# A conditional ternary feed-forward kernel: x and the result kept block by block in HBM, one row per partition

## The chip, the cores and the metric

The kernel runs on one core of one Trainium2 chip. The core has five engines with a queue each: TensorE (PE, with its weight loads shown as PEld), VectorE (DVE), ScalarE (ACT), GpSimd (POOL) and SyncE (SP). Sixteen DMA engines move data between HBM, the memory outside the core, and SBUF, the memory of 128 partitions inside it; PSUM holds the sums of matmuls. The metric is the device time of one execution in microseconds (us), the median over several runs. Arranging the inputs and the result on the host isn't part of it.

## The reference

x has 128 samples of 64 channels and 512 tokens in float32, 16.8 MB. Each sample picks one 64 x 64 matrix from a table of 200, and then all go through a feed-forward layer with ternary weights; the result is quantized with one scale over the whole tensor and added to x.

```python
w = weights[conditions]                          # (128, 64, 64)
z = einsum('bct,bcd->bdt', x, w)                 # per sample
W1q, W2q = ternarize(W1), ternarize(W2)          # alpha * sign(W) where |W| > 0.05 max|W|
h = gelu(einsum('bsd,hd->bsh', z, W1q) + b1)     # 512 -> 2048
y = einsum('bsd,hd->bsh', h, W2q) + b2           # 2048 -> 512
scale = max(abs(y)) / 7 + 1e-8                   # one number for all of y
q = clip(round(y / scale), -7, 7) * scale
return x + q
```

Since the scale needs the largest element of all of y, no part of the result can be written before the last block's y is known.

## The kernel before, in words

Two samples fill the 128 partitions (2 x 64 channels): a pair. Four pairs make a block, so there are 16 blocks of 1 MB of x, 8 KB per partition. A tile of x in SBUF is 128 partitions x 4 pairs x 512 tokens, and half a block is two pairs.

The kernel has three stages. At the start, SP loads both weight matrices (8 KB rows per partition, `nat1`, `nat2`) with block 0 of x between them; thresholds and ternary weights are made, while POOL gathers the conditional matrices row by row (`fetch`) and lays them into a block-diagonal `diag` (`place`). In the middle, block after block, PE mixes each pair of the next block with `diag` and runs the two layers over 16 hidden chunks; blocks 2 to 12 use a scheme with seven products in place of eight (`seven`). The y of blocks 0 to 14 stays in SBUF (`ys`), that of block 15 in PSUM. At the end, the scale is found, and for each half of each block ACT rounds y to int8, DVE multiplies by the scale and adds x, in place, and POOL issues the store.

x is therefore read twice: once for the layers and once for the final addition. The functions that load it all issue on SP:

- `load_x` (line 104): a whole block into a tile of the pool `big`, as two loads of half a block each.
- `half_x` (line 112) and `split_x` (line 118): half a block into a tile of the pool `half`.
- `quarter_x` (line 743): one pair, for blocks 2 to 13, into one of two slots of `x_quarters`.
- `lend` (line 819): one pair of blocks 3 and 4, for the final addition, into the room of a weight tile that is no longer read.

For the final addition, blocks 0 to 2 are loaded during the last block's layers, 3 and 4 by `lend`, 5 and 6 by `load_x`, 7 to 9 by `split_x`, and 10 to 15 by `load_x` inside the final loop. The order of issue on every engine is the order of the program (`InOrder`, line 55, is the line that all records carry). What decides when one of these loads starts is the tile it is given: SP waits there until the earlier user of the room has finished, be it DVE, PE or the store of a y. The names x_blk and out_blk (lines 98 and 99) are views of x and of the result in which one partition's row of a block is four pieces of 2 KB that lie 256 KB apart.

Of the kernel before, what the change touches and what calls it, by code (L numbers as in the profile page):

```python
# [40 lines left out]
P = 128  # L41
# [17 lines left out]
def tile_cond_ternary_ffn(  # L59
# [12 lines left out]
    pe, act, dve, pool, sp = (  # L72
        InOrder(tc, e) for e in (nc.tensor, nc.scalar, nc.vector, nc.gpsimd, nc.sync)
    )
    B, C, T = x.shape
    S, _, D = weights.shape
    NT = T // P
    NH = W1.shape[1]
    assert 2 * C == P and 2 * D == P and C == D and W1.shape == (P, NH, NT, P)
    PAIRS = 4  # L80
    BLK = PAIRS * P
    NB = B // (2 * PAIRS)
    NG = 4
    GH = NH // NG
    WCH = GH * T
# [9 lines left out]
    ps_h = ctx.enter_context(tc.tile_pool(name="ps_h", bufs=2, space=PSUM))  # L95
    ps_y = ctx.enter_context(tc.tile_pool(name="ps_y", bufs=1, space=PSUM))

    x_blk = x.rearrange("(n j p) c t -> n (p c) j t", j=PAIRS, p=2)
    out_blk = out.rearrange("(n j p) c t -> n (p c) j t", j=PAIRS, p=2)

    def pair_of_pairs(h):
        return slice(h * PAIRS // 2, (h + 1) * PAIRS // 2)

    def load_x(n):

        xt = big.tile([P, PAIRS, T], F32, tag="big", name=f"xt_{n}")
        for h in range(2):
            js = pair_of_pairs(h)
            sp.dma_start(out=xt[:, js, :], in_=x_blk[n][:, js, :])
        return [xt[:, pair_of_pairs(h), :] for h in range(2)]  # L110

    def half_x(n, h):

        xt = half.tile([P, PAIRS // 2, T], F32, tag="half", name=f"xt_{n}_{h}")
        sp.dma_start(out=xt, in_=x_blk[n][:, pair_of_pairs(h), :])
        return xt

    def split_x(n):

        return [half_x(n, h) for h in range(2)]  # L120
# [14 lines left out]
    for g in range(NG):  # L135
        w = big.tile([P, GH, T], F32, tag="big", name=f"nat1_{g}")
        for ks in PIECES[g]:
            sp.dma_start(out=w[:, ks, :], in_=W1f[:, g * GH :, :][:, ks, :])
        nat1.append(w)
    x_next = load_x(0)  # L140
    b1t = const.tile([P, NH], F32)
    sp.dma_start(out=b1t, in_=b1)
    for g in range(NG):
# [57 lines left out]
    def parts(n):  # L201
        return [big.tile([P, NT, BLK], F32R, tag="big", name=f"x{k}_{n}") for k in range(2)]
# [54 lines left out]
    def flat(w):  # L257
        return w.rearrange("p a b -> p (a b)")
# [115 lines left out]

    ymax = const.tile([P, NB + 1, PAIRS], F32)
    alpha = {}
# [12 lines left out]
    def widen2(n, hc):  # L389
        if n == 0 and hc < NH - LAG:  # L390
            w = w2f[hc % 4]
        elif n == NB - 1 and hc == NH - 1:

# [241 lines left out]

    w1t = big.tile([P, NH, T], F8, tag="big", name="w1t")
    x_next = load_x(1)

    def kept(t, g, tiles):
# [3 lines left out]
    for hc in range(NH - LAG):  # L643
# [21 lines left out]
        if hc in (5, 7, 9, 11):  # L665
            j = (hc - 5) // 2
# [3 lines left out]
    x_next, two_next, fetched = [], [], []  # L670
# [10 lines left out]
    extra = {}  # L681
# [29 lines left out]
    def parts7(n):  # L711

        return (
            big.tile([P, 2, NT, HALF], F32R, tag="big", name=f"xb_{n}"),
            [big.tile([P, 4, 2, HALF], F32R, tag="big", name=f"xt{k}_{n}") for k in range(2)],
            half.tile([P, 2, 2, HALF], F32R, tag="half", name=f"xl_{n}"),
        )
# [24 lines left out]

    def quarter_x(n, j):

        sp.dma_start(out=extra["x"][:, j % 2, :], in_=x_blk[n][:, j, :])

    def product(out, w, b, first):
        for c in range(2):
# [65 lines left out]

    steps = [(n, hc) for n in range(NB) for hc in range(NH)]
    again = []
    dying = [flat(t).bitcast(F32).rearrange("p (j t) -> p j t", j=PAIRS) for t in (w1t, w2t)]

    def lend(t, n, hc):

        if n == NB - 1 and hc % (NH // PAIRS) == NH // PAIRS - 1:
            j = hc // (NH // PAIRS)
            sp.dma_start(out=dying[t][:, j, :], in_=x_blk[3 + t][:, j, :])

    def eight(s):

        n, hc = steps[s]
        if s + 1 < len(steps):
            ahead = steps[s + 1]
            if ahead[0] not in SEVEN:  # L830
                widen1(*ahead)
                lend(0, *ahead)
            else:
                for g in (2, 3, 0):
                    widen7(0, g)
        widen2(*steps[s + 1 - LAG])
        lend(1, *steps[s + 1 - LAG])
        if n + 1 < NB:
            if hc == 0:
                if n + 1 == SEVEN[0]:  # L840
                    extra["x"] = half.tile([P, 2, T], F32, tag="half", name="x_quarters")
                    for j in range(2):
                        quarter_x(n + 1, j)
                else:
                    x_next.append(load_x(n + 1) if n + 1 < NB - 1 else split_x(n + 1))
                two_next.append(parts7(n + 1) if n + 1 in SEVEN else parts(n + 1))
            if 2 <= hc < 2 + PAIRS:
                fetched.append(fetch(n + 1, hc - 2))
            if 7 <= hc < 7 + PAIRS:
                place(hc - 7, fetched[hc - 7 - PAIRS])  # L850
# [10 lines left out]
        if n + 1 < NB and 8 <= hc < 8 + PAIRS:  # L861
            j = hc - 8
            if n + 1 in SEVEN:
                condition7(n + 1, j, extra["x"][:, j % 2, :], two_next[-1])()
                if j + 2 < PAIRS:
                    quarter_x(n + 1, j + 2)
            else:
                condition(n + 1, j, pair_of(x_next[-1], j), two_next[-1])
            cond[n + 1] = two_next[-1]
# [17 lines left out]
    def pair(n, k, finish):  # L887
# [14 lines left out]
        def behind(i):  # L902
# [16 lines left out]
            if i == 2:  # L919
                if parting:  # L920
                    parting.pop()()
                if k == 1:
                    quarter_x(n + 1, 0)
                    quarter_x(n + 1, 1)
                if k in (4, 5):
                    quarter_x(n + 1, k - 2)
                widen2(*steps[s])
                if not leaves:
                    widen7(ahead, 2)
# [23 lines left out]
    while s < len(steps):  # L953
        n, hc = steps[s]
# [14 lines left out]
    n = NB - 1  # L969
    widen2(n, NH - 1)  # L970
    lend(1, n, NH - 1)
    again += [[t[:, pair_of_pairs(h), :] for h in range(2)] for t in dying]
    for _ in range(2):
# [30 lines left out]
    for n in range(NB):  # L1004

        while len(xs) < min(AHEAD + 3 * n // 2, NB):
            xs.append(load_x(len(xs)))
        for h in range(2):


            q = quant[:, h * PAIRS // 2 : (h + 1) * PAIRS // 2, :]
            if n < NB - 1:
                y = res = ys[n][:, pair_of_pairs(h), :]
                act.activation(flat(q), flat(y), AF.Identity, scale=inverse)
                dve.scalar_tensor_tensor(
                    flat(y), flat(q), scale, flat(xs[n][h]), ALU.mult, ALU.add
                )
            else:
                res = xs[n][h]
                for k in range(PAIRS // 2):  # L1020
                    y = ypsum[n][h * PAIRS // 2 + k]
                    act.activation(q[:, k, :], y, AF.Identity, scale=inverse)
                    dve.scalar_tensor_tensor(
                        res[:, k, :], q[:, k, :], scale, res[:, k, :], ALU.mult, ALU.add
                    )
            pool.dma_start(out=out_blk[n][:, pair_of_pairs(h), :], in_=res)


_INS = [
# [9 lines left out]

LAID_OUT = {
    "itok_B_1_198": lambda a: a.reshape(-1, 2).T.repeat(P // 2, axis=0),
    "L0_ffn_W1": lambda a: a.reshape(-1, P, a.shape[1] // P, P).transpose(3, 0, 2, 1),
    "L0_ffn_b1": lambda a: a.reshape(-1, P).T,
# [25 lines left out]
```

## Time and profile before

| What | Value |
|---|---|
| Median of 3 runs | 1064.39 us (1062.46 to 1064.63) |
| The profiled execution, time | 1062.89 us |
| The profiled execution, span from first to last instruction | 1061.0 us |
| PE busy | 986.1 us, 93% |
| DVE, ACT, POOL busy | 58%, 58%, 59% |
| DMA, load queue (q1): packets, MB, share of 16 engines | 19872, 42.25, 12.0% |
| DMA, queue of POOL (q0): packets, MB, share of 16 engines | 6656, 18.88, 4.6% |
| Half-block loads of x (36), from issue to landing | 7.2 us, median |
| Stores of y (30), from issue to landing | 12.9 us, median |
| Quarter loads of x (48), from issue to landing | 2.6 us, median |

A row of the profile names the engine, the operation, what it writes and what it reads, with tile numbers left out. Times in a timeline or a chain are us from the span's start, and the number after it is the length in us. In the lines of 40 slices each digit is the busy share of a slice in tenths. The queue q1 carries what SP issues, q0 what POOL issues: gathers, and at the end the stores. A packet is what a DMA engine takes from a queue at a time. The landing of a DMA is when its semaphore has its full count.

### The profile page before, as it was taken

Reading aid. Unit: us, or ns where it says so; the run is one execution under the profiler, and the core shown is the slowest. Engines: PE = TensorE matmul, PEld = TensorE weight load, DVE = VectorE, ACT = ScalarE, POOL = GpSimd, SP = SyncE. Lnnn points to the kernel's source line nnn. Section 1 sums busy time; section 2 is a strip of 40 time slices with the busy share of each in tenths; the row PEclk is TensorE's granted clock in tenths of the full one; section 3 lists DMA queues with packets and bytes.
Section 4 is the critical chain, followed back from the end, with each engine's and each line's share of the span. In section 5 each row is a group of like instructions: output and inputs, shape, how many; then the busy total and the mean of one; then the engine's idle time right before and its main releaser. Section 6 shows DMA issues by size and latency. Waiting matters only on the chain.

```text
span 1061.0 us, 16715 instructions
## 1 busy us (share of the span) xinstructions
PE 986.1 (93%) x5760; PEld 864.0 (81%) x5761; DVE 610.9 (58%) x1078; ACT 611.4 (58%) x1040; POOL 628.2 (59%) x1016
## 2 busy tenths in 40 slices
PE   8999999999999999999999999999999999999400
PEld 5887889999999999999999999999998888888300
DVE  7896645666656565666656565666645224232682
ACT  7974445666666565656666565656655433343481
POOL 6855656676766667676766767676664435333242
PEclk9999999999999999999999999999999999999755
DMA  9100000101000010101000010100001010041899
GB/s 361 57 20 3 23 22 12 34 6 31 15 22 23 14 32 7 39 6 32 15 22 23 14 32 5 40 6 30 16 22 43 3 40 6 1 149 33 301 413 372
DMA packets 26611, 62.20 MB, mean 59 GB/s; under 512 B 3488, under 2 KB 3488, under 8 KB 25760
## 3 DMA queue, kind: packets, MB, share of 16 engines
q1 hardware_dynamic: 19872, 42.25, 12.0%
q0 software_dynamic: 6656, 18.88, 4.6%
q8 instruction: 47, 0.77, 0.3%
q14 instruction: 36, 0.29, 0.1%
HBM read 44.34 MB, written 16.78 MB: 58 GB/s over the span
## 4 chain that ended last, share of the span: by engine, by line
PE 87%; DVE 4%; DMA 3%; ACT 2%; issue 1%; POOL 1%; SPq 1%; POOLq 0%; DVEq 0%; ACTq 0%
PE py L55 42%; PE xy L55 16%; PE ph L55 13%; PE z L55 12%; PE pc L55 5%; DMA xt<-in_x 3%; DVE h L55 1%; DVE y L55 1%; ACT diag L55 1%; DVE terns L55 1%; POOL wg L55 1%; ACT junk L55 1%; SPq L55 1%; DVE junk L55 1%; DMA wg<-in_L_cond_weights,rows 1%
## 5 line engine op out<-in xcount | busy, mean ns | idle before, releaser
L55 PE MATMUL py<-wf,h 128*128 128x512 f32 x2048 | 531.2, 395 | 0.9 <-ACT h L55 0.7
L55 PEld LDWEIGHTS py<-wf,h 128*128 128x128 f32 x2048 | 365.4, 189 | 65.1 <-DVE y L55 2.0
L55 DVE TENSOR_TENSOR h<-ring,h 128x512 fp32r<-128x512 f32 x252 | 194.7, 775 | 182.1 <-ACT h L55 182.1
L55 POOL CAST wf<-w2t 128x512 fp32r<-128x512 fp8e4 x242 | 173.7, 718 | 154.4 <-PE py L55 142.4
L55 ACT ACTIVATE ring<-ring,b1t,alpha_w 128x512 f32<-128x512 f32 x176 | 144.3, 820 | 97.7 <-DVE ring L55 97.7
L55 POOL CAST wf<-w1s 128x256 fp32r<-128x256 fp8e4 (+1 forms) x264 | 134.4, 514 | 108.9 <-PE xy L55 80.5
L55 POOL CAST wf<-w1t 128x256 fp32r<-128x256 fp8e4 (+1 forms) x240 | 156.7, 658 | 56.7 <-PE ph L55 45.2
L55 ACT CAST h<-ring 128x512 fp32r<-128x512 f32 x256 | 158.9, 621 | 8.3
L55 PE MATMUL ph<-x,wf 128*128 128x512 f32 (+1 forms) x648 | 157.6, 388 | 2.8 <-ACT x L55 2.1
L55 PEld LDWEIGHTS ph<-x,wf 128*128 128x128 f32 x648 | 119.8, 188 | 28.8 <-issue 2.5
L55 ACT ACTIVATE ring<-ph,b1t,alpha_w 128x512 f32<-128x512 f32 x80 | 62.3, 779 | 139.6 <-PE ph L55 139.5
L55 DVE TENSOR_TENSOR ring<-xy,ring 128x256 f32<-128x256 f32 (+1 forms) x176 | 97.3, 553 | 64.2 <-PE xy L55 64.2
L55 PEld LDWEIGHTS xy<-xt,wf 128*128 128x128 f32 x704 | 107.6, 189 | 14.1
L55 PE MATMUL xy<-xb,wf 128*128 128x256 f32 x704 | 112.4, 281 | 0.0
L55 PE MATMUL xy<-xt,wf 128*128 128x256 f32 x704 | 111.8, 282 | 0.0
L55 PEld LDWEIGHTS xy<-xb,wf 128*128 128x128 f32 x704 | 102.2, 190 | 7.9
L55 ACT COPY ring<-xy 128x256 f32<-128x256 f32 x176 | 65.1, 370 | 67.7 <-PE xy L55 67.7
L55 PE MATMUL z<-xt,wf 128*128 128x256 f32 x704 | 98.3, 282 | 0.0
L55 ACT COPY ring<-z 128x512 f32<-128x512 f32 x88 | 51.7, 588 | 73.9 <-DVE h L55 72.5
L55 PEld LDWEIGHTS z<-xt,wf 128*128 128x128 f32 x704 | 90.2, 190 | 0.0
L55 DVE TENSOR_TENSOR xt<-x_quarters,xt 128x512 fp32r<-128x512 f32 x44 | 33.8, 768 | 91.1 <-ACT xt L55 91.1
L55 POOL DMA_INDIRECT wg<-in_L_cond_weights,rows x64 | 73.5, 1148 | 11.7 <-issue 4.4
(103 smaller groups left out, 851.4 us busy)
## 6 DMA issues: line engine op xcount, KB each, us to landing
xt<-in_x SPq DMA_DIRECT2D x36, 512.0 KB, 7.2
out<-y POOLq DMA_DIRECT2D x30, 512.0 KB, 12.9
x_quarters<-in_x SPq DMA_DIRECT2D x48, 256.0 KB, 2.6
nat<-in_L_ffn_W SPq DMA_DIRECT2D x6, 1024.0 KB, 10.2
nat<-in_L_ffn_W SPq DMA_DIRECT2D x3, 512.0 KB, 9.0
wg<-in_L_cond_weights,rows POOLq DMA_INDIRECT x64, 2.7
w1t<-in_x SPq DMA_DIRECT2D x4, 256.0 KB, 2.6
w2t<-in_x SPq DMA_DIRECT2D x4, 256.0 KB, 2.6
```

The lines of the kernel that those rows point to most:

```text
L55: return lambda *args, **kw: self._tc.keep_in_program_order(make(*args, **kw))
```

## The change

In HBM, x and the result become arrays of 16 blocks x 128 partitions x 4 pairs x 512 tokens, so that a partition's row of a block is 8 KB in one piece, and that of half a block 4 KB. The host puts x in this order and the result back. In the kernel, `load_x` issues one load of 1 MB in place of two of 512 KB, except for block 0 at the start, where it keeps two (`halves`). The other loads and the stores stay as they are in number and size, with the views replaced by plain indexing. A pair's load now takes 2 KB out of every 8 KB.

```diff
-    B, C, T = x.shape
-    S, _, D = weights.shape
+    S, C, D = weights.shape
+    T = x.shape[-1]
...
-    NB = B // (2 * PAIRS)
+    NB = x.shape[0]
+    B = NB * PAIRS * 2
...
-    x_blk = x.rearrange("(n j p) c t -> n (p c) j t", j=PAIRS, p=2)
-    out_blk = out.rearrange("(n j p) c t -> n (p c) j t", j=PAIRS, p=2)
...
-    def load_x(n):
+    def load_x(n, halves=False):
 
         xt = big.tile([P, PAIRS, T], F32, tag="big", name=f"xt_{n}")
-        for h in range(2):
-            js = pair_of_pairs(h)
-            sp.dma_start(out=xt[:, js, :], in_=x_blk[n][:, js, :])
+        if halves:
+            for h in range(2):
+                js = pair_of_pairs(h)
+                sp.dma_start(out=xt[:, js, :], in_=x[n][:, js, :])
+        else:
+            sp.dma_start(out=xt, in_=x[n])
         return [xt[:, pair_of_pairs(h), :] for h in range(2)]
...
-        sp.dma_start(out=xt, in_=x_blk[n][:, pair_of_pairs(h), :])
+        sp.dma_start(out=xt, in_=x[n][:, pair_of_pairs(h), :])
...
-    x_next = load_x(0)
+    x_next = load_x(0, True)
...
-        sp.dma_start(out=extra["x"][:, j % 2, :], in_=x_blk[n][:, j, :])
+        sp.dma_start(out=extra["x"][:, j % 2, :], in_=x[n][:, j, :])
...
-            sp.dma_start(out=dying[t][:, j, :], in_=x_blk[3 + t][:, j, :])
+            sp.dma_start(out=dying[t][:, j, :], in_=x[3 + t][:, j, :])
...
-            pool.dma_start(out=out_blk[n][:, pair_of_pairs(h), :], in_=res)
+            pool.dma_start(out=out[n][:, pair_of_pairs(h), :], in_=res)
...
+    "x": lambda a: a.reshape(-1, 4, P, a.shape[2]).transpose(0, 2, 1, 3),
...
-    shape = inputs["x"].shape
+    shape = arrays["in_x"].shape
...
-    return r.results[0]["out_0"]
+    return r.results[0]["out_0"].transpose(0, 2, 1, 3).reshape(inputs["x"].shape)
```

## The prediction

> **What bounds the kernel now.** I read the forty slices first, then the chain that ended last, then the stretches of the tail with their DMA traffic by queue.
>
> ```profile
> PE   8999999999999999999999999999999999999400
> DMA  9100000101000010101000010100001010041899
> GB/s 361 57 20 3 23 22 12 34 6 31 15 22 23 14 32 7 39 6 32 15 22 23 14 32 5 40 6 30 16 22 43 3 40 6 1 149 33 301 413 372
> ```
>
> A slice is 26.5 us. TensorE sets the pace in 36 of them while the DMA engines idle; only the first slice and the last three are different. In the last three the DMA engines are the busy ones. The chain shows the change of hands near 988 us, and how it ends:
>
> ```profile
> 987.39 0.63 ACT h L55
> ...
> 1018.95 3.54 SPq L55
> ...
> 1022.60 1.33 SPq L55
> 1023.93 0.04 issue
> 1023.98 27.00 DMA xt<-in_x
> ```
>
> The last load of x takes 27.00 us from its issue to its landing, although 512 KB move in 1.3 us at 400 GB/s: it stands in a queue. SP itself spends 3.54 us and 1.33 us on single issues here (elsewhere 0.33 to 0.46)[...]. So the tail is bounded by bytes over the DMA rate, not by any one transfer. The whole tail (985 to 1062 us), by queue, and then three pure stretches and the mixed one (packets, MB, rate; and per queue the share of the 16 engines):
>
> ```profile
> DMA packets 10738, 28.60 MB, mean 371 GB/s; under 512 B 880, under 2 KB 880, under 8 KB 10736
> q0 software_dynamic: 4608, 16.78, 53.6%
> q1 hardware_dynamic: 6128, 11.80, 41.6%
> ```
>
> Start, 4 to 8 us, weights in 8 KB rows, loads only:
>
> ```profile
> DMA packets 228, 1.66 MB, mean 416 GB/s; under 512 B 22, under 2 KB 22, under 8 KB 28
> ```
>
> 994 to 999.5 us, x in 2 KB rows, loads only; 1020 to 1030 us, loads and stores; 1050 to 1054 us, stores only:
>
> ```profile
> DMA packets 1130, 2.19 MB, mean 397 GB/s; under 512 B 70, under 2 KB 70, under 8 KB 1129
> ...
> DMA packets 1488, 4.15 MB, mean 415 GB/s; under 512 B 123, under 2 KB 123, under 8 KB 1488
> q0 software_dynamic: 743, 2.70, 66.0%
> q1 hardware_dynamic: 745, 1.45, 37.3%
> ...
> DMA packets 462, 1.67 MB, mean 418 GB/s; under 512 B 53, under 2 KB 53, under 8 KB 462
> ```
>
> What to see: 2 KB packets alone run at 397 GB/s, 8 KB packets at 416, stores at 418 (their queue already joins two 2 KB pieces into one 4 KB packet: 32 stores of 0.524 MB in 4,096 packets, the rest of the 4,608 being 32 x 16 completions), and the mixture at 415. In the mixture the two queues take equal numbers of packets, 743 and 745, so bytes go 2.70 to 1.45.
>
> [...] the trace has 416 over 397, 4.8%. [...] the best stretches here stay at 416 to 420.[...] a 256 KB load of x lands in 2.6 us in the trace of before, so the joined loads save no queue time worth counting when transfers overlap.
>
> **The change, part by part.** Every TensorE, DVE, ScalarE and GpSimd instruction stays, in its order. On SP, 11 pairs of 512 KB loads become single 1 MB loads (block 1, block 14, and in the tail blocks 0, 5, 6 and 10 to 15); the other loads stay separate. Rows are 8 KB for these, 4 KB for half-block loads and stores, 2 KB for the quarter loads, now 8 KB apart.
>
> Fit of a packet, from the two load-only rates, per engine (rate/16): 2,048 B in 82.5 ns at 397, 8,192 B in 315.1 ns at 416. Slope 232.6 ns/6,144 B = 37.9 ps/B, overhead 5.0 ns. So 4 KB would run at 409 GB/s, and no packet overhead at all at 422.
>
> (1) Start. Block 0 of x (1 MB, behind 4 MB of weights, 12.9 to 15.5 us) moves at 409 in place of about 380 to 397: up to 0.15 us sooner. The chain there runs through the last gather (landed 13.91 us) and POOL's copies into diag, not through x: 0. If the 4 KB packets delay that gather instead, by two packets at 80 ns, +0.2 us; its bytes mostly passed before block 0's did. I take 0.
>
> (2) Middle. Block 1 is loaded at 42.0 us, lands at about 46.8 and is first read at 64.9; the joined load lands no later than its second half did. The 48 quarter loads land in 2.6 us and no engine but SP waits for one. PE's 18 us of other work is the cover, so the cost is 0; with the cover gone PE would wait the 4.8 us of the landing. What their new 8 KB spacing does to their speed the trace doesn't show as such; weights, in 8 KB rows spaced 32 KB, ran at 416. Even double time (5.2 us) fits in the two steps of 3.6 us between issue and use.
>
> (3) Tail, first loads. Blocks 5, 6 and the first half of 7 (2.62 MB, 0.12 of it moved by 988) are queued by 988.8 us; the next load is issued only at 992.50 us, when PE frees its buffer. Before: 2.19 MB from 988 to 994, mean 365 (the slices fall to 188 GB/s around 991), the last 0.31 MB at 397, so done at 994.8. After: 2.50/0.416 = 6.0 us, at 994.0. Saved 0.8 us if the hollow at 991 goes, 0.3 if it comes again. The load issued at 992.50 moves from about 993.3, so DMA isn't left idle.
>
> (4) The next five half loads (2.62 MB, 4 KB rows): 6.6 us at 397, 6.4 at 409. Saved 0.2.
>
> (5) All the rest, 28.60 - 0.12 - 2.50 - 2.62 = 23.36 MB, from 1001.4 us to the end of movement at about 1058.6, 57.2 us, mean 408. The steady rate is 415.5 and cannot pass 422 by the fit: between 0 and 57.2 x (1 - 415.5/422) = 0.9 us. I take 0.9, as both sides have fewer pieces: loads a quarter, stores half. Two hollows (336 GB/s from 1003 to 1005, 348 from 1012.5 to 1013.5) cost 0.4 and 0.15 us; between 0 and 0.55 is saved. I take 0.55, because the overfull load queue, the likeliest cause, has a quarter of the packets after.
>
> (6) The end. A joined load frees DVE only when both halves are in. Now DVE takes the last half at 1051.07 and the last store is issued at 1052.78; its data still stand behind others until about 1058. Joined alone would put the last store one DVE piece (1.41 us) later, 1054.2, and still ahead of that backlog: cost 0. But the round by packets now gives loads 8 KB against 4 KB, so two thirds of the rate (277 GB/s). Block 10 lands at about 1006; 11 to 15 wait for freed buffers (stores of blocks 0 to 2) and DVE, are queued by about 1017, and land by about 1028 in place of 1051. Late instead are the stores, which fill the queue to the end. POOL waits for its eighth-last store, DVE doesn't wait for POOL. No engine idles the DMA: 0, and if DMA were left idle, up to 1.4 + 0.7 us.
>
> Sum: 0.8 + 0.2 + 0.9 + 0.55 = 2.45 us off the profiled 1062.89 us (span 1061.0 and 1.89 around it). The median, 1064.39, lies 1.5 above that execution; I take the same 2.45 from it: 1061.9 us.
>
> **Rivals.** *Capped mixture:* the two queues already hide each other's packet overhead (415 against 397 alone), so (5) gains only 415 to 418, 0.4 us, and the hollows return: 0.3 + 0.2 + 0.4 = 0.9, 1063.5 us. For it: the mixture stands within 0.7% of stores alone. Against: hollows fall where load packets crowd.
>
> *Slow stores:* a store now writes 4 KB of every 8 KB of the result, where it wrote solid 256 KB runs. 16.78 MB at 418 take 40.1 us. The gain is eaten when stores run at 16.78/42.6 = 394; below 375 the kernel is more than 0.2% slower. At 370, 45.4 us: +5.3 - 2.45 = +2.8, 1067.2 us. For it: nothing in the trace writes so. Against: 8 KB rows read from 32 KB apart ran at 416.
>
> *More gain:* all traffic at 422 moves 28.60 MB in 67.8 us in place of 70.5 (988 to 1058.5), and the ragged end (1057 to 1059.5) sharpens by 1: -3.7, 1060.7 us.
>
> *No effect,* were 8 KB rows cut to 2 KB anyway: excluded, 200 of the packets from 4 to 8 us are of 8 KB.
>
> **How the numbers follow.** Forecast 0.58 (of which 0.05 fall short of the bound), capped mixture 0.21, slow stores 0.14 (0.13 slower, the rest same), more gain 0.07. A measurement of this kernel tells about 0.2%, 2.1 us, from no change. Faster 0.60, same 0.27, slower 0.13. The range leaves out most of the slow stores and the far end of the gain: 1060.3 to 1065.2; the forecast's own is 1060.9 to 1062.6.
>
> **What would show it.** Right: load-only stretches after 988 at 409 to 416 with packets of 8 KB; loads near two thirds of the bytes while both run; block 15 landed by about 1030; no SP issue over 1 us; DVE through by about 1040 and the last 25 us stores alone near 420. Wrong: stores alone below 400, DMA share below 0.9 anywhere from 988 to 1056, PE starting its first ph later than 20.63 us, or a PE wait on x_quarters.

## The result and the profile after

The changed kernel takes 1068.23 us (median of 7 runs, 1066.53 to 1069.81) against 1064.43 us before: a ratio of 1.0038, interval 1.0029 to 1.0048. It is slower by 3.8 us, where 2.5 us less were forecast, and outside the range.

The profiled execution of the changed kernel takes 1068.34 us, span 1066.5. Its forty slices, 26.7 us each:

```profile
PE   8999999999999999999999999999999999999200
DMA  9100000100000000000000000000001010131997
GB/s 363 54 20 3 23 22 8 38 6 30 15 22 23 14 32 14 31 6 31 14 22 23 20 26 14 32 5 30 16 22 44 2 41 5 34 115 40 341 421 311
```

PE still sets the pace in the same 36 slices, and the DMA engines are the busy ones in the first and the last three. The traffic of the tail (985 to 1068 us) has as many bytes in fewer packets: the load queue has 2,160 in place of 6,128. Below stand the whole tail and then, in order, loads alone (994 to 999.5 us), loads and stores (1020 to 1030), stores alone (1050 to 1054):

```profile
DMA packets 6771, 28.61 MB, mean 345 GB/s; under 512 B 752, under 2 KB 752, under 8 KB 5744
q0 software_dynamic: 4608, 16.78, 49.9%
q1 hardware_dynamic: 2160, 11.80, 36.4%
...
DMA packets 549, 2.27 MB, mean 412 GB/s; under 512 B 63, under 2 KB 63, under 8 KB 482
...
DMA packets 768, 4.25 MB, mean 425 GB/s; under 512 B 80, under 2 KB 80, under 8 KB 418
q1 hardware_dynamic: 384, 2.87, 67.8%
q0 software_dynamic: 384, 1.38, 33.8%
...
DMA packets 464, 1.67 MB, mean 418 GB/s; under 512 B 56, under 2 KB 56, under 8 KB 464
```

These rates are as forecast or better: 412 GB/s where the kernel before had 397, 425 where it had 415, 418 where it had 418. The two queues still take equal numbers of packets, 384 each, so loads have two thirds of the bytes. The chain that ended last (start, length, what) has other links, though. It no longer ends in a load of x but in stores waiting for stores:

```profile
1024.48 2.49 DVE y L55 x2
1026.98 0.05 issue
1027.03 14.74 DMA out<-y
...
1042.32 9.44 DMA out<-y
...
1052.28 0.55 POOLq L1071
```

The view's chain stops there, at 1052.83 us, while the DMA engines are still at work.

The last packet of the last store ends at 1061.39 us, and yet the span goes on to 1066.5. What stands there is in the instructions of the program's last line: SP waits for the last landings (EVENT_SEMAPHORE), GpSimd's queue (POOLq) has an instruction that the profile calls DRAIN, then all engines meet. First of the kernel before, then of the changed one (count, shortest/median/longest in ns, first and last start in us):

```profile
L1067 SPq EVENT_SEMAPHORE  x11: 17/28/28, 1059.6 to 1061.0; - x11
L1067 POOLq DRAIN  x3: 40/102/7461, 1052.8 to 1060.8; - x3
```

```profile
L1071 SPq EVENT_SEMAPHORE  x11: 17/28/28, 1061.7 to 1066.4; - x11
L1071 POOLq DRAIN  x3: 40/102/13426, 1052.3 to 1066.2; - x3
```

SP's first wait ends with the last landing, at 1059.6 and 1061.7 us. The long DRAIN begins with the issue of the last store; it took 7.461 us before, to 1060.22, 0.6 us after the landing, and 13.426 us after, to 1065.71, 4.0 us after it.

So the 5.45 us between the two spans part in three:

| Stretch | Before | After | Difference, us |
|---|---|---|---|
| Start to the scale known (start of DVE's reciprocal) | 996.59 | 998.02 | 1.43 |
| From there to the end of the last packet | 62.63 | 63.37 | 0.74 |
| From there to the end of the span | 1.82 | 5.10 | 3.28 |

The first isn't the change's. Between 70 and 110 us the granted TensorE clock was 1.00 in the one profile and 0.96 in the other (half speed for 3.4 us at 86 us). In the 18 profiles of this document the scale is known at 996.4 to 997.1 us in the five without such a dip and at 997.7 to 998.7 us in the 13 with it, in both orders of x. The other two rows make 4.0 us, near the 3.8 of the medians. Of these the 3.28 us behind the last packet are the greater part; the 0.74 us come from one profile each, and the kernel before with one small instruction more (`e8_before_wait` below) has 63.20 us in that row, so the 0.74 is not clear of the spread.

### The profile page after: what moved, and what is told of

Its sections match the earlier page's. It is cut to its first block, busy times and chain, and to the rows that moved or that the text cites. A ratio compares the mean times of both kernels' runs of the same rounds, so it can differ in the third digit from the quotient of the medians.

```text
span 1066.5 us, 16692 instructions
## 1 busy us (share of the span) xinstructions
PE 988.2 (93%) x5760; PEld 865.2 (81%) x5761; DVE 608.9 (57%) x1078; ACT 611.3 (57%) x1040; POOL 620.3 (58%) x1016
## 4 chain that ended last, share of the span: by engine, by line
PE 87%; DVE 5%; DMA 3%; ACT 2%; POOL 1%; issue 1%; POOLq 0%; ACTq 0%; DVEq 0%
PE py L55 41%; PE xy L55 16%; PE ph L55 13%; PE z L55 12%; PE pc L55 5%; DMA out<-y 2%; DVE y L55 2%; ACT diag L55 1%; DVE h L55 1%; DVE terns L55 1%; POOL wg L55 1%; ACT junk L55 1%; DVE junk L55 1%; DMA wg<-in_L_cond_weights,rows 1%; ACT w2t L55 1%
## 5 line engine op out<-in xcount | busy, mean ns | idle before, releaser
L55 PEld LDWEIGHTS py<-wf,h 128*128 128x128 f32 x2048 | 365.5, 189 | 65.2 <-DVE y L55 2.0
```

What stands on the lines that cost most here:

```text
L55: return lambda *args, **kw: self._tc.keep_in_program_order(make(*args, **kw))
```

## The experiments

Theory A blamed the order of loads and stores for the long DRAIN, theory B the 4 KB pieces of a store, theory C the movement of the data itself. A piece is a run of bytes of one partition that lies in one stretch in HBM. "The scale" stands for the moment at which it is known, as in the table.

**Each half of the change alone.** `e1_x_only`:

```diff
-            pool.dma_start(out=out[n][:, pair_of_pairs(h), :], in_=res)
+            pool.dma_start(out=out_blk[n][:, pair_of_pairs(h), :], in_=res)
```

> Only x is kept block by block; the result keeps its old order, so a store is 2 KB pieces again. Theory A (the loss is POOL's last DRAIN, and it is long because the loads come first and a longer queue of stores stands behind the last store's issue): the loads still come first, so the DRAIN stays at 12 us or more, ends over 3 us after the last data packet, and the kernel is 0.3% slower than before, 1067.5 us or more. Theory B (the DRAIN is long because a store is made of 4 KB pieces): DRAIN ends about 1 us after the last packet as before, and the time is 1063 to 1065 us. Theory C (the loss is in the movement of the data, slow stores at an 8 KB pitch): stores alone at 419 GB/s or more, last packet earlier than in the changed kernel by 1 us, and the time within 1 us of before.

`e2_result_only` is the kernel before with only this line (and the result's shape on the host) the other way round.

> Only the result is kept block by block; x keeps its old order and its loads of half a block in 2 KB pieces. Theory A: loads share the rate as before, the queue of stores at the end is as before, the DRAIN ends about 1 us after the last packet, time 1063 to 1065 us. Theory B: the DRAIN ends over 3 us after the last packet, time 1067 us or more. Theory C: last packet later than before by 1 us, time 1065 to 1068 us.

Measured: x alone 1067.01 us, ratio 1.0035 (1.0022 to 1.0047); the result alone 1067.34 us, 1.0028 (1.0018 to 1.0037). Each half loses nearly as much as both, for different reasons. With x alone the DRAIN ends 0.6 us after the last landing, but the last packet comes 65.2 us after the scale, 2.5 later than before: the loads are done early (landed by 1037.2 us), the stores run alone for 26 us, and with 2 KB pieces their rate falls from 413 GB/s (1040 to 1045 us) to 398, 355 and 381 in the next three stretches of 5 us. The changed kernel's 4 KB pieces ran at 416 to 419 from 1040 to 1055 us. The pieces alone don't explain it, since the kernel before ran the same 2 KB pieces alone at 416 to 420 from 1050 to 1056 us; why they turn slow after some 10 us alone stays open. With the result alone the last packet comes at 63.0 and the DRAIN ends 3.98 us after the landing. A fell; of C a part is true for x alone; B seemed to stand (1067.34 us, where it said 1067 or more).

**Stores taken from GpSimd.** The same line with `(sp if n >= 12 else pool)` and later `(sp if n >= 8 else pool)`:

> The changed kernel with the stores of blocks 12 to 15 (the last 8 of 32) issued by SP in place of POOL. Theories A and B: POOL's DRAIN ends before the last data, so the end comes about 1 us after the last packet; 3 to 3.5 us faster than the changed kernel, 1064.5 to 1065.5 us. Theory C: as slow as the changed kernel, 1067.5 to 1069 us.

> The changed kernel with the stores of blocks 8 to 15 (the last 16 of 32) issued by SP, so that POOL's own stores have landed some 10 us before the end. Theory D (POOL's last DRAIN ends a few us after the last landing of POOL's own stores when these are of 4 KB pieces): the DRAIN ends before the last data, the span ends under 2 us after the last packet, and the kernel is 2.5 to 3.5 us faster than the changed one, 1064.5 to 1065.5 us. Theory E (the DRAIN waits for something that comes after all data of the core, whoever issued them): 4 to 5 us after the last packet again, 1067.5 us or more.

With 8 of 32 stores on SP nothing is gained: 1068.04 us, 1.0040 (1.0026 to 1.0054). All three theories had a forecast for this, but the last of GpSimd's stores landed at 1061.20 us, later still than SP's (1057.65), and the DRAIN ended 3.65 us after that. So GpSimd wasn't done early, and the run was no test of A and B. With 16 on SP GpSimd's last store lands at 1047.44 and its DRAIN, begun at 1025.4 and 25.320 us long, is over at 1050.76, 3.32 us after that landing:

```profile
L1071 SPq EVENT_SEMAPHORE  x11: 17/28/28, 1050.5 to 1060.9; - x11
L1071 POOLq DRAIN  x3: 40/102/25320, 1025.4 to 1060.7; - x3
```

The span ends 1.3 us after the last packet, and the time is 1064.31 us, 1.0003 (0.9994 to 1.0012) of before. The data aren't faster for it: 63.3 us from the scale. So it is the end of the DRAIN that costs the 3 to 4 us. That the move to SP brings nothing of its own is checked below with the kernel before.

**A wait ahead of the DRAIN.** Behind the last store, in the changed kernel and in the one before, GpSimd writes one column into the tile that this store reads, so that it has to wait for the store's landing first:

```diff
+    pool.memset(res[:, 0, :1], 0.0)
```

> The changed kernel with one small memset on POOL behind the last store, into the tile that this store reads, so that POOL waits for the store's landing before its DRAIN. If the DRAIN is long because it starts with stores under way and looks for their end only now and then: it is now under 0.5 us, the end is about 1 us after the landing, 1064.5 to 1065.5 us. If the DRAIN is work that POOL still has to do (theory B's kind, in the order of its queue): the memset or the DRAIN ends as late as before, about 4 us after the last packet, 1067.5 to 1069 us.

> The kernel before with the same small memset on POOL behind the last store as in the run that waited before the DRAIN. If a DRAIN behind stores of 2 KB pieces has nothing to wait for: under 0.5 us, and the time is that of before plus 0 to 0.5 us. If a DRAIN begun after the landing takes about 8 us whatever the pieces: 8 us again, 1071 us or more, and the long DRAIN would be the memset's doing or a matter of when it starts, not of the pieces.

The changed kernel with the wait, then the kernel before with it:

```profile
L1072 POOLq DRAIN  x3: 40/102/8055, 1062.3 to 1070.9; - x3
```

```profile
L1068 POOLq DRAIN  x3: 40/102/1277, 1061.7 to 1063.5; - x3
```

Times 1073.24 us, 1.0084 (1.0066 to 1.0101), and 1065.68 us in one run. The memset itself ran in 0.1 us at the landing, and still 8.055 us of DRAIN followed. So the DRAIN isn't idle waiting: here it took 8.055 us with every store landed, and 3.98 us of it were left after the landing in the changed kernel, where it starts early. With the old stores it takes a sixth, 1.277 us.

**Pieces and counts.** Stores cut into quarters of a block (`out[n][:, h * PAIRS // 2 + j, :]`), the last 8 in the old order (this kernel leaves part of the result's rows in another order than it should), those of blocks 0 to 14 joined to a whole block (`out=out[n], in_=ys[n]`), and the kernel before with 16 stores on SP:

> The changed kernel with each store cut into two, one per pair: 64 stores of 256 KB, one piece of 2 KB per partition, 8 KB apart. If the size of a piece (4 KB) makes the DRAIN long: it ends within 0.6 us of the last landing, span end under 2 us after the last packet. If one piece per partition, as against two, makes it long: 4 us after the landing again.

> The changed kernel with the last 8 stores (blocks 12 to 15) in the old order of the result, so of 2 KB pieces, two per partition; these blocks' rows of the result stand in another order than the rest. If the form of the last stores decides the DRAIN: it ends within 0.6 us of the last landing. If what POOL issued before counts too (24 stores of 4 KB pieces): 2 to 4 us after it.

> The changed kernel with the two stores of each of blocks 0 to 14 joined into one of 1 MB, 8 KB pieces; 17 stores in place of 32. If the DRAIN grows with the size of a piece: it ends 6 to 8 us after the last landing. If it grows with the number of stores of pieces of 4 KB or more: 3.3 us or less, as with 16 such stores. The data end about 1 us later than in the changed kernel, since a store starts only when both halves of a block are done.

> The kernel before with the stores of blocks 8 to 15 issued by SP, nothing else changed. With 2 KB pieces POOL's DRAIN was over within 0.6 us of the last landing, so there is nothing to save there: within 1 us of before, 1063.3 to 1065 us. If moving the stores to SP brings something of its own (a better sharing of the DMA engines), it shows here as more than 1 us.

Times: 1069.42, 1069.54 and 1068.58 us in one run each, and 1064.81 us, 1.0003 (0.9995 to 1.0012). From the scale to the last packet they took 66.9, 64.0, 63.7 and 64.1 us; the quarter stores lose their time there and not in the DRAIN. The last of the four also shows that stores on SP bring the kernel before nothing, and it brought theory B down: its stores have 2 KB pieces, and the DRAIN ended 3.32 us after GpSimd's last landing, exactly as with 16 stores of 4 KB pieces (landing at 1036.07 us, DRAIN over at 1039.39):

```profile
L1067 POOLq DRAIN  x3: 40/102/18192, 1021.2 to 1063.7; - x3
```

Sorted by number of DMAs the durations fall on a line. The pieces per engine in the table are an estimate of mine, from the shapes in the kernel and the packets of GpSimd's queue in the traces before and after. Each of the 64 gathers, 128 rows of 256 B, made 16 packets of 2 KB, so eight rows in one, and each of the 32 stores made 128 packets of 4 KB; every one of the 96 DMAs also made 16 packets of 4 B, counted as completions. Shared evenly over 16 engines that makes 8 pieces and a completion, 9, for a gather or a store of one piece per partition, and 17 for a store of two, where a joined packet is counted by its pieces. That joined pieces count singly is assumed; the packets don't show it.

| Run | DMAs of GpSimd | Pieces per engine, completions counted | DRAIN's end after GpSimd's last landing, us | per DMA, ns |
|---|---|---|---|---|
| 16 stores on SP (changed; before) | 80; 80 | 720; 848 | 3.32; 3.32 | 41.5 |
| whole-block stores | 81 | 729 | 3.36 | 41.5 |
| 8 stores on SP | 88 | 792 | 3.65 | 41.5 |
| changed; result only; last 8 old | 96 | 864; 864; 928 | 3.98; 3.98; 3.97 | 41.4 |
| before; x only | 96 | 1,120 | 0.59; 0.59 | - |
| quarter stores | 128 | 1,152 | 0.95 | - |

Theory H is my conjecture from these counts. Call a DMA of GpSimd retired when GpSimd has no more to do for it. H supposes that the DRAIN goes through every DMA that has not been retired, the 64 gathers of the middle too, so that the measured 41.5 ns for each are left after the last landing; and that DMAs are retired earlier only when their pieces fill a room of some 1,020 per engine. By the estimate the kernel before gets there at its 27th store (1,018 pieces before it, 1,035 with it), and its trace has a stall at this store. The timeline of GpSimd in the kernel before (in brackets the idle time ahead):

```profile
1038.94 0.73 POOL L55 DMA_DIRECT2D out<-y  x1 [1.23 <-DMA out<-y]
1042.89 1.46 POOL L55 DMA_DIRECT2D out<-y  x2 [3.22 <-DMA out<-y]
```

The 27th, at 1042.89, goes out 2.60 us after the landing that it waits for (that of the eighth store before it, at 1040.29); others follow theirs by 0.5. With x alone it is the 27th again, by 2.60, and with quarter stores the 50th (1,017 pieces before it, 1,026 with it), by 3.01. The number of DMAs doesn't decide: the stall is at the 91st of GpSimd's DMAs in the first two and at the 114th with quarter stores, while the changed kernel has 96 and no stall. In the kernel before the DMA engines moved 412 to 418 GB/s from 1040 to 1046 us, across the stall, so it cost no movement.

Two more figures of these traces fit. The stores that hadn't landed when the stall began are 13 before and with x alone, 22 with quarter stores; at 41.5 ns each that makes an estimate of 0.54 and 0.91 us for the last column, where 0.59 and 0.95 were measured. And the stall grows with the DMAs that had landed by then: 83 of them and 2.05 us beyond the usual 0.55, 106 of them and 2.46 us, some 24 ns each.

**The count crossed by gathers.** Only the lines below distinguish the two kernels from the changed one, and only the limit, 16 or 20, from each other (not shown: the rest of the gather's arguments and the line that makes the spare tile):

```diff
+    def spare_fetch():
+        if len(spares) < 16:
+            spares.append(1)
+            pool.indirect_dma_start(out=spare[:, :], ...)
...
+                elif k in (6, 7):
+                    spare_fetch()
```

> The changed kernel with 16 more gathers on POOL in the middle (into a spare tile that nothing reads), so 112 DMAs of POOL in place of 96. Theory H (the last DRAIN goes through every DMA of POOL that hasn't been retired, 41.5 ns each after the last landing; they are retired earlier only when their pieces fill a fixed room, between 1,018 and 1,026 pieces per DMA engine by the runs so far): 64 x 9 + 16 x 9 + 32 x 9 = 1,008 pieces, room not full, DRAIN ends 112 x 0.0415 = 4.65 us after the last landing, no late store, the kernel 0.5 to 1 us slower than the changed one, 1068.5 to 1069.5 us. Theory B (the pieces' form): 4.0 us as in the changed kernel.

> The same with 20 more gathers: 1,044 pieces. Theory H: the room is full at the 30th store (64 x 9 + 20 x 9 + 29 x 9 = 1,017 pieces before it, 1,026 with it), this store is issued some 2.5 us after its lane is free in place of 0.5, and only about 10 DMAs are left to retire, so the DRAIN ends 0.4 to 0.6 us after the last landing although there is more work: 3 us faster than the changed kernel, 1064.5 to 1066 us. Theory B: 4.0 us after the landing, 1068 us or more.

With 16 more, then with 20 more, and GpSimd's timeline of the latter:

```profile
L1086 SPq EVENT_SEMAPHORE  x11: 17/28/28, 1060.6 to 1065.9; - x11
L1086 POOLq DRAIN  x3: 40/102/14096, 1051.1 to 1065.7; - x3
```

```profile
L1086 POOLq DRAIN  x3: 40/102/8747, 1053.5 to 1062.7; - x3
```

```profile
1048.63 0.53 POOL L55 DMA_DIRECT2D out<-y  x1 [0.74 <-DMA out<-y]
1052.45 0.54 POOL L55 DMA_DIRECT2D out<-y  x1 [3.29 <-issue]
1053.00 1.05 POOL L55 DMA_DIRECT2D out<-xt  x2
```

With 16 the DRAIN ends at 1065.19, 4.63 us after the landing at 1060.57 (forecast 4.65), and no store is late. With 20 the 30th store, at 1052.45, comes 3.1 us after the landing it waits for, and the DRAIN ends at 1062.23, 0.46 us after the last landing (10 stores left at the stall: 0.42 by the estimate above). Times 1067.87 us, 1.0035 (1.0022 to 1.0049), and 1065.17 us, 1.0005 (0.9996 to 1.0013): four gathers more make the kernel 2.7 us faster. The first is 0.6 us under its forecast; its data came a little sooner (63.2 us from the scale). H foretold the DRAIN's end (4.63 and 0.46 us after the landing) and the place of the stall (the 30th store); what GpSimd does for each DMA, and whether there is a room that fills, isn't visible.

**The data and a version for use.** The forecast had the two hollows in the rate go. In the changed kernel the first one went deeper. The stretches are 2 us long, the last number is GB/s, and the one ahead of it the busy share of the DMA engines. The kernel before from 5 to 11 us after its scale, then the changed one, then the one with blocks 5 and 6 in halves, each at the same distance:

```profile
1001.60:1003.60 2.00, 0.00 (x0) 0.00 (x0) 1.98 (x3) 1.80 (x3) 0.99 (x2) 0.50 1.05 387
1003.60:1005.60 2.00, 0.00 (x0) 0.00 (x0) 1.98 (x3) 1.80 (x3) 1.19 (x2) 0.50 1.02 362
1005.60:1007.60 2.00, 0.00 (x0) 0.00 (x0) 2.00 (x2) 1.84 (x2) 1.19 (x2) 0.50 1.04 415
```

```profile
1003.00:1005.00 2.00, 0.00 (x0) 0.00 (x0) 1.98 (x3) 1.79 (x3) 0.77 (x2) 0.50 1.06 356
1005.00:1007.00 2.00, 0.00 (x0) 0.00 (x0) 1.98 (x3) 1.80 (x2) 0.82 (x2) 0.50 0.88 268
1007.00:1009.00 2.00, 0.00 (x0) 0.00 (x0) 2.00 (x2) 1.85 (x2) 0.97 (x2) 0.50 0.87 303
```

```profile
1003.70:1005.70 2.00, 0.00 (x0) 0.00 (x0) 1.98 (x3) 1.80 (x3) 0.79 (x2) 0.50 1.05 422
1005.70:1007.70 2.00, 0.00 (x0) 0.00 (x0) 1.98 (x3) 1.80 (x3) 0.81 (x2) 0.50 1.06 432
1007.70:1009.70 2.00, 0.00 (x0) 0.00 (x0) 2.00 (x2) 1.84 (x2) 0.98 (x2) 0.50 0.96 381
```

It is no accident of one profile. From 3 to 11 us after the scale 2.44 to 2.81 MB were moved in the 11 profiles with blocks 5 and 6 in 8 KB pieces, 3.11 to 3.33 in the three with them in halves, and 3.09 to 3.24 in the four with x in its old order.

Four kernels were run on it: all whole-block loads as halves, 16 stores on SP (`halves=True` as the default); block 10 alone in halves, with whole-block stores for blocks 3 to 13, 16 stores' worth on SP (`load_x(len(xs), len(xs) == 10)`); the same with blocks 5 and 6 in halves too (`load_x(len(again), True)`); and the changed kernel with blocks 5 and 6 alone in halves.

> The kernel with the stores of blocks 8 to 15 on SP, and now every whole-block load as two halves again, in 4 KB pieces (block by block layout kept). Theory F (the hollow in the rate 3 to 11 us after the scale is known, 276 to 336 GB/s, comes from the 8 KB packets of block 10 meeting the first stores): the hollow shrinks to that of before (355 to 388 GB/s) or less, the last packet comes 0.5 to 1 us sooner after the scale than with whole blocks (62.3 to 62.8 us in place of 63.3), time 1063.3 to 1063.9 us, faster than before by 0.3 to 0.8 us. Theory G (the hollow comes from the new place of x in HBM, whatever the piece): as deep as with whole blocks, 1064 to 1065 us.

> A version for use: the changed layout; stores of blocks 8 to 15 on SP; block 10 loaded in halves, the other whole blocks in one load; the stores of blocks 3 to 13 a whole block each (8 KB pieces), the others half a block. By theory H POOL's DRAIN (64 gathers and 11 stores) is over long before the end. By theory F the hollow stays small. With 8 KB pieces on both sides the mixture and the stores should run at 425 to 427 GB/s in place of 416 to 420, so the last packet 61.5 to 62.3 us after the scale is known (62.6 before): 1062.8 to 1063.8 us, 0.05 to 0.15% faster than before.

> The version for use, with blocks 5 and 6 in halves too (4 KB pieces), so that no 8 KB load runs before block 11's. If the hollow 3 to 11 us after the scale comes from the 8 KB loads of blocks 5 and 6 (or from their early end): it goes, as in the run with all loads in halves (406 to 421 GB/s), and the last packet comes 61.3 to 61.9 us after the scale; 1063.0 to 1063.6 us, 0.1 to 0.15% faster than before. If the hollow needs 4 KB pieces in all loads, those of blocks 11 to 15 included: it stays at 250 to 360 GB/s, 1064 us.

> The changed kernel with blocks 5 and 6 alone in halves. If the 8 KB loads of blocks 5 and 6 make the hollow: 380 GB/s or more from 3 to 11 us after the scale, in place of 276 to 388. If block 10's 8 KB load makes it as well: as deep as in the changed kernel. The end stays long (DRAIN 4.0 us after the last landing), since POOL's DMAs are the same 96.

Times in this order: 1063.70 us, 0.9995 (0.9986 to 1.0004); 1063.97 us, 0.9993 (0.9984 to 1.0001); 1064.05 us, 0.9999 (0.9991 to 1.0007); 1068.37 us in one run. From the scale to the last packet: 62.46, 62.14, 62.45 and 62.70 us. Block 10 in halves didn't remove the hollow (254 GB/s from 7 to 9 us after the scale), blocks 5 and 6 in halves did, in two kernels out of three wholly and in the third but for one stretch at 307. But a hollow then stands where their own loads run: 234 to 246 GB/s from 7 to 5 us ahead of the scale, where the 8 KB loads of the changed kernel made 410. So halves move it rather than remove it, and theory F as it was put, block 10's packets, fell. What the hollow is stays open. Whole-block stores did raise the rate, to 428 GB/s in mixture (1020 to 1030 us) and 416 to 429 alone, but the last us are ragged (317 GB/s from 1056 to 1058 us, then 16). The gains of 0.05 to 0.15% that were forecast for the two mixed versions didn't come: none of these versions is shown to be faster than the kernel before. The first three undo the loss.

## Why the prediction was wrong

**The bound of the tail, right.** It is a queue of bytes, and the two queues' packets went one for one (384 each from 1020 to 1030 us). Loads got two thirds there (2.87 of 4.25 MB), all were landed by 1036.9 us in place of 1051.0 (1028 was forecast), and DVE was through at 1039.8.

**Steps (1) and (2), right.** PE's first ph (a matmul of the first layer) started at 20.57 us (20.63 before), no engine but SP waited for a quarter load, though these now land in 3.1 us in place of 2.6.

**Steps (3) and (4), size off.** 1.0 us was forecast. Integrated from 11 us before the scale to 3 after, the changed kernel moved 0.17 MB more, 0.4 us. The 8 KB loads began slowly (237 GB/s from 989 to 991 us; the kernel before had 338 at the same distance from its scale) and then ran at 408 to 424.

**Step (5), wrong in one term.** The mixture came out at 425, even above the 422 of the fit, and over the time from 11 to 40 us after the scale this is worth 0.25 MB, 0.6 us, where 0.9 was forecast. But I took the hollows as the work of an overfull queue, which was my reading of SP's long issues and not shown, let them go and counted 0.55 us for it. SP's longest issue did fall, from 6.75 to 1.54 us, and still the hollow from 3 to 11 us deepened, by 0.46 MB or 1.1 us; so an overfull queue is no longer its likeliest cause. At 61 us after the scale both kernels had moved 28.3 MB: the whole gain was spent. One of the signs named for a wrong forecast was here, a DMA share below 0.9 (0.88 and 0.87 from 1005 to 1009 us).

**Step (6), the failure.** "No engine idles the DMA: 0" was beside the point. I took the saving off the whole time, so that the 1.8 us after the last packet stood in it as a constant without a reason, and the sum stopped at the last byte. The change also alters how many pieces GpSimd's DMAs have: by the estimate 17 to 9 per store and engine, from 1,120 in all to 864. Before, GpSimd stalled at the 27th store, which went out 2.60 us after the landing it waits for in place of 0.5, while other stores moved, and the DRAIN ended 0.6 us after the last landing. After, no store stalled, and the DRAIN ended 4.0 us after it; behind the last packet that makes 3.3 us more than before. That some 80 DMAs were retired in the stall, and all 96 at the end after the change, is H's reading. The last 0.3 MB also took 0.7 us longer (279 GB/s and a DMA share of 0.68 from 1058 to 1060 us); why isn't shown, nor that it is more than spread.

**The miss as a sum.** 2.45 us less were forecast, and from the scale on 4.0 us more were measured, 6.5 us apart. Half of that, 3.3 us, is the end of step (6). The other half, about 3.2, is movement: 0.6 in steps (3) and (4), 0.3 in the mixture and 1.7 in the hollow of step (5), 0.7 in the last bytes. So the DRAIN explains why the kernel got slower, and the hollow, whose cause is open, is about half of why the movement brought no gain.

**Two readings.** The prediction sets SP's issues of 3.54 and 1.33 us against 0.33 to 0.46 elsewhere, but from 1009 to 1018 us five others took 1.31 to 1.76 us, and the last one 6.75. It puts the end of movement at about 1058.6 us; the last packet ended at 1059.2.

**The rivals.** *Slow stores* had the right sign and the wrong mechanism: stores with 4 KB of every 8 KB ran at 418, and it was the old 2 KB pieces that turned slow when left alone for long (355 to 398). *Capped mixture* was wrong on the rate, 425 for 418, but right in that the hollow came again. *More gain* and *no effect* didn't come. No rival looked behind the last packet, though the stall of 3.22 us at 1042.89 and the DRAIN of 7.5 us stood in the trace of before. The measured 1068.2 us lie near the 1067.2 of *slow stores* by luck.

## What to carry to other kernels

The end of a kernel isn't its last byte: look at what each engine does between the last landing and the end, and how many DMAs stand behind it. In this kernel the pieces of a store decided whether GpSimd stalled earlier, while other stores moved, or had 4.0 us of DRAIN left after the last landing; giving half of the stores to SP took those off the end (DRAIN over at 1050.76 us, last packet 1.3 us ahead of the end of the span), and so did 20 gathers more (0.46 us left). And faster loads that come first leave the stores to run alone, so what the stores do alone has to be measured too.

## What the runs showed of the hardware

- Where GpSimd had not stalled, its DRAIN ended 41.3 to 41.5 ns per DMA of GpSimd after the last landing of these (80 DMAs 3.32 us with 16 stores on SP, 96 3.98 in the changed kernel, 112 4.63 with 16 gathers more). Begun at the landing, behind the added memset in the changed kernel, it took 8.055 us for 96, twice that.
- GpSimd stalled once, and its DRAIN ended 0.46 to 0.95 us after the last landing, in the kernel before, with x alone, with quarter stores and with 20 gathers more: where the pieces of its DMAs, by the estimate above, rose from 1,017 to 1,026 or from 1,018 to 1,035 per engine. That store went out 2.6 to 3.1 us after the landing it waits for, in place of 0.5. At an estimated 1,008 (16 gathers more) or fewer no store was late.
- Packets of one engine took 84 ns for 2 KB, 159 for 4 KB, 309 for 8 KB on the load queue of the changed kernel (medians): worked out from these, 390, 412 and 424 GB/s over 16 engines. GpSimd's stores alone, in stretches of 5 us, ran at 413 and then 355 to 398 with 2 KB pieces (x alone, from 1040 us; 416 to 420 in the kernel before, 1050 to 1056 us), at 416 to 419 with 4 KB (the changed kernel, 1040 to 1055 us).
- Quarter loads of 2 KB pieces landed in 2.6 us (median) when the pieces were next to each other, in the kernel before, and in 3.1 us when 8 KB apart, in the changed one.
